# Attention, then a mixture of experts, on one core: the order of work inside a group of blocks is turned round

## The chip, the core and the metric

The kernel runs on one core of one Trainium2 chip. The metric is the device time of one execution in microseconds (us). The kernel before takes 1038.86 us (median of 3 runs, 1036.79 to 1040.83).

Five engines work side by side, each through its own queue in order: TensorE (PE in the profile, with PEld for its weight loads), VectorE (DVE), ScalarE (ACT), GpSimd (POOL) and SyncE (SP), which here only issues transfers (DMAs).

## What is computed

A transformer layer in fp32 on 2048 tokens of 128 numbers. The first half is causal attention with 16 heads of 64, the second a gated mixture of 8 experts with 2 chosen for each token, plus a shared expert. Cut to what matters here:

```python
x = L0_attn_x                                   # (1, 2048, 128)
qkv = einsum('bse,ehd->bshd', layernorm(x), qkv_w) + qkv_b
q, k, v = split(qkv, 3, axis=-1)
logits = where(causal, einsum('bqhd,bkhd->bhqk', q, k) / sqrt(64), large_negative)
probs  = softmax(logits, axis=-1)
attn   = einsum('bhqk,bkhd->bqhd', probs, v)
x = x + einsum('bqhd,hde->bqe', attn, out_w) + out_b
x = x + shared_ffn(layernorm(x)) + sum over the two best experts of weight * expert_ffn(layernorm(x))
```

## The kernel before, in words

**Pairs and steps.** Heads are taken in pairs j = 0 to 7. The 2048 query rows are taken in steps m = 0 to 7 of 256 rows: rows (128-row blocks) i = 2m and 2m+1. Within a pair the steps come in the order `turns` (L384): 2, 7, 0, 6, 1, 5, 3, 4. A step m has 2m+2 blocks of 128 keys.

**Scores.** `score_units` (L394) makes units of at most 512 keys for one row i and both heads. TensorE multiplies (L429, tile `sc`). VectorE scales or masks, writes `row` and takes the maximum (L440, and L444 for the last piece of a row), then the negative maximum `neg` (L458). ScalarE takes the exponential in place over the whole row (L461), one instruction for each head. I write sc_11_2 for the third unit of row 11, exp_11 for the two exponentials of row 11, neg_11 for its negative maximum.

**Turning the probabilities.** The product with V needs them transposed. There are two ways. Steps m = 4 to 7 are *by slabs* (L390): all but their last blocks are transposed within 32x32 squares by VectorE (L496), written to DRAM by SyncE (L500, tile `stage`) and read back (L514, tile `turned`); the last two or four blocks are turned by TensorE ahead of time into `tail` (`turn_last`, L527). All blocks of steps m = 0 to 3 are turned by TensorE: `turn` (L516) makes up to four transposes into one PSUM tile `tr` (L522), and ScalarE copies that to SBUF (L525, tile `pT`, six buffers). I write tr_0_1 for block 1 of step 0, and "the copy of tr_0_1" for that copy.

**Product, division, projection.** `times_v` (L547) multiplies one block with V into the accumulator `av` (L554). The sums of the exponentials are inverted (L480), transposed (L483, tile `inv`), and spread over 64 partitions by way of DRAM: GpSimd issues the write `invd` (L485) and, in `spread` (L562), the two reads `inb` (L567), which wait for the write. `divide` (L573) multiplies `av` by `inb` on VectorE (L575, tile `aT`). `project` (L578) multiplies `aT` by the output weights on TensorE (L581, tile `po`), and VectorE adds `po` to `xr` (L582). I write T:inv_0, inb_0, av_0, aT_0 and po_0 for those of step 0.

**Fill.** The projections to K, Q and V of the next pair are single units (`pq` L352 and `pv` L369) that are put between the rest from the queue `fill`. ScalarE moves K and V out of PSUM (L364, L376), VectorE Q (L362).

**PSUM.** All tiles but `av` come from one ring of six (tag "r"): a new `sc`, `tr`, `po`, `pq` or `pv` waits until the tile taken six places earlier has been read.

**What sets the order.** TensorE and VectorE work in the order in which the program is written (L614). ScalarE, GpSimd and SyncE are ordered by a planner when the kernel is built; the order is fixed from then on. The loop over steps (L665) splits each step into groups of blocks. A slab step has three groups: its tail, and two halves of the rest. Other steps have groups of three blocks. In each group the written order is:

1. a fill unit (steps that are not by slabs)
2. the turns of this group's blocks (`turned`, L533)
3. the projection of the step that ended before (`finish`, L656)
4. the product with V of the group *before* (kept in `last`); a slab step takes what is kept and its own blocks at once
5. a fill unit (slab steps), and slab transposes that are due (`turn_slabs`)
6. score units of a step that comes two or four steps later, by the counts in `runs`

Of the kernel before, what the change touches and what calls it, by code (L numbers as in the profile page):

```python
# [16 lines left out]
P = 128  # L17
# [6 lines left out]
def attention_then_moe(  # L24
# [58 lines left out]
    def load_wq(j, engine):  # L83
        wq_of[j] = norm.tile([P, 3, 2, D], F32, tag="wq", name=f"wq_{j}", bufs=3)
        engine.dma_start(wq_of[j], qkv_w[:, :, 2 * j : 2 * j + 2, :])
# [7 lines left out]
    with nc.allow_non_contiguous_dma(reason="1024 numbers"):  # L93
# [16 lines left out]
        fill=MASKED,  # L110
# [104 lines left out]
    def route_units(blocks):  # L215
# [34 lines left out]
        def turn_row(t0):  # L250
            part = blocks[t0 : t0 + 4]
            pt = psp.tile([P, 512], F32, tag="r", name=f"pt_{k0}_{t0}")
            for t, b in enumerate(part):
                nc.tensor.transpose(pt[:, ts(t, P)], row[:, t0 + t, :E], ident)
            for t, b in enumerate(part[::2]):
                nc.scalar.copy(zT[:, b * P : (b + 2) * P], pt[:, ts(t, 2 * P)])
            in_zT.update(part)
# [77 lines left out]
                    )  # L335
                    no_order("sent", ins)

        turns = [lambda t0=t0: turn_row(t0) for t0 in range(0, n, 4)]
        return [statistics, normed, None, *turns, None, logits, None, best1, best2, ranks]


    attn = tc.tile_pool(name="attn", bufs=2)
# [2 lines left out]
    def qkv_units(j):  # L345
        kT = pool.tile([P, S], F32, tag="kT", name=f"kT_{j}")
        qT = [None] * NG
        vt = pool.tile([P, NT, P], F32, tag="vt", name=f"vt_{j}")

        def qk_unit(s, n):  # L350
            pq = psp.tile([P, 512], F32, tag="r", name=f"pq_{j}_{s}_{n}")
            nc.tensor.matmul(  # L352
                pq,
                wq_of[j][:, s, :, :],
                xnT[:, ts(n, 512)],
                start=True,
                stop=True,
            )
            bias = bqk[:, s, j : j + 1]
            if s == 0:  # L360
                qT[n] = pool.tile([P, 512], F32, tag=f"qT{n}", name=f"qT_{j}_{n}", bufs=1)
                nc.vector.tensor_scalar_add(qT[n], pq, bias)  # L362
            else:
                nc.scalar.activation(kT[:, ts(n, 512)], pq, AF.Identity, bias=bias)  # L364

        def v_unit(g):
            pv = psp.tile([P, 4, P], F32, tag="r", name=f"pv_{j}_{g}")
            for t in range(4):
                nc.tensor.matmul(  # L369
                    pv[:, t, :],  # L370
                    xnT[:, ts(4 * g + t, P)],
                    wq_of[j][:, 2, :, :],
                    start=True,
                    stop=True,
                )
            nc.scalar.copy(vt[:, ts(g, 4), :], pv)  # L376

        q, k = ([lambda s=s, n=n: qk_unit(s, n) for n in range(NG)] for s in range(2))
        return (kT, qT, vt), q, k, [lambda g=g: v_unit(g) for g in range(NG)]
# [10 lines left out]
    def by_slabs(m):  # L390

        return (2 * m) // 4 * 4 if 2 * m >= NT // 2 else 0
# [78 lines left out]
    def turn_slabs(most, age=True, due=False):  # L471


        for t in to_turn:
            t[-1] -= age
        while to_turn and (to_turn[0][-1] < 0 or not (age or due)) and most:
            j, m, q, h, sums, _ = to_turn.popleft()
            if h == 1:
                inv = inv_of[j, m]
                nc.vector.reciprocal(inv[:, 2 * q : 2 * q + 2], sums)  # L480
                if q == 1:

                    nc.vector.transpose(inv, inv)  # L483
                    invd_of[j, m] = dram.tile([32, P], F32, tag=f"inv{m}", name=f"invd_{j}_{m}")
                    nc.gpsimd.dma_start(  # L485
                        invd_of[j, m].rearrange("n (a i) -> a n i", a=4),
                        inv,
                    )
            X = by_slabs(m) * 32
            if not X:  # L490
                continue
            most -= 1
            if q == 0 and h == 0:
                staged_of[j, m] = dram.tile([P, 16 * X], F32, tag=f"stage{m}", name=f"stage_{j}_{m}")
            row = rows_of[j, m][q][:, h, : 4 * X]
            nc.vector.transpose(row, row)  # L496
            row = row.rearrange("p (b x) -> p b x", b=4)
            to = staged_of[j, m].rearrange("(b i) (c x) -> i b c x", i=32, c=16)
            for a in range(4):
                ins = nc.sync.dma_start(to[:, :, 8 * q + 4 * h + a, :], row[ts(a, 32)])  # L500
                no_order(f"stage_{j}_{m}", ins)
# [106 lines left out]
    def scores_of(n):  # L608
        if n >= len(steps):
            return deque()  # L610
        j, m = steps[n]
        return deque(score_units(j, m, *qkv[j][0][:2]))
# [12 lines left out]
        u()  # L625
        turn_slabs(2)
    fill, later = deque(), deque()
    last = []
    ending = None

    shared_w = []
# [1 line left out]
    def load_shared():  # L633
        for k, w in enumerate((w_gate, w_up, w_down)):
            t = norm.tile([P, 3 * P], F32, tag="wq", name=f"shared_{k}", bufs=3)
            if k < 2:
                t = t[:, :F]
                nc.sync.dma_start(t, w[:, NE, :])
            else:
                t = t.rearrange("p (c e) -> p c e", c=NFC)  # L640
                for c, (f0, fn) in enumerate(FCH):
                    nc.sync.dma_start(t[:fn, c, :], w[f0 : f0 + fn, NE, :])
            shared_w.append(t)
# [18 lines left out]
                    blocks = [b for m in batch for b in (2 * m, 2 * m + 1)]  # L662
                    routes.append(deque(route_units(blocks)))

    for n, (j, m) in enumerate(steps):  # L665
        at = n % NM
        if at == 0 and j + 1 < NP:
            qkv[j + 1] = qkv_units(j + 1)


            _, q, k, v = qkv[j + 1]
            fill.extend([*k, q[3], *v])
            later.extend([q[1], q[0], q[2]])
            if j + 2 < NP:
                load_wq(j + 2, nc.sync)
            while j and blank:
                nc.sync.dma_start(blank.popleft(), mask[:, :ROW].unsqueeze(1).to_broadcast([P, 16, ROW]))
        if at == 0 and j == NP - 1:
            load_shared()
        if at == 5 and later:  # L680
            assert not fill
            fill.extend(later)
            later.clear()
        if at == 6 and j + 1 < NP:
            assert not fill
        near = by_slabs(m)
        coming = scores_of(n + (4 if near else 2))
        if n == 0:
            coming.extend(scores_of(3))

        if near:
            groups = [list(range(near, 2 * m + 2))]
            groups += [list(range(k, k + near // 2)) for k in range(0, near, near // 2)]
            runs = [3, 3, len(coming) - 6]
        else:
            groups = [list(range(k, min(k + 3, 2 * m + 2))) for k in range(0, 2 * m + 2, 3)]
            half = len(coming) // 2
            runs = {1: [len(coming)], 2: [2 * (half // 2), half], 3: [0, half, half]}[len(groups)]
        for k, group in enumerate(groups):
            if fill and not near:  # L700
                fill.popleft()()
            turn_slabs(1)
            now = [turned(j, m, b) for b in group]
            if k == 0:
                spread(j, m)
            if ending is not None:
                finish(*ending)
                ending = None
            route_on()
            ready, last = (last + now, []) if near else (last, now)  # L710
            for t in ready:
                jt, mt, b = t[:3]
                times_v(*t, qkv[jt][0][2])
                if b == (by_slabs(mt) or 2 * mt + 2) - 1:
                    assert ending is None
                    ending = (jt, mt, divide(jt, mt))
            if fill and near:
                fill.popleft()()
            turn_slabs(1, age=False, due=True)
            if near and k == 0 and n + 2 < len(steps):  # L720
                turn_last(*steps[n + 2])
            if n == 0 and k == 0:
                turn_last(*steps[1])
            if n == 0 and k == 1:
                load_turned(*steps[1])
            if near and k == 1 and n + 2 < len(steps):
                load_turned(*steps[n + 2])
            for _ in range(runs[k] if k < len(groups) - 1 else len(coming)):
                if coming:
                    coming.popleft()()  # L730
    assert not last
    finish(*ending)
    assert len(routes) == 2
    attn.__exit__(None, None, None)
# [309 lines left out]
```

## Time and profile before

| what | value |
|---|---|
| median of 3 runs | 1038.86 us (1036.79 to 1040.83) |
| the profiled execution | 1043.9 us, of which its span is 1042.2 us |
| mean granted TensorE clock | 0.971 |
| PE busy | 949.6 us (91%) |
| DVE busy | 745.1 us (71%) |
| ACT busy | 541.3 us (52%) |
| POOL busy | 211.3 us (20%) |
| DMA | 205.33 MB, mean 197 GB/s |

The span has three parts. Up to about 42 us the input is normalised and turned. From there to about 860 us the eight pairs follow, about 101 us each in the middle (one and the same wait of a score unit ends at 444.00 us in one pair and at 544.74 us in the next). The rest is the mixture of experts.

How to read it: "busy" for TensorE is made of records whose ends are modelled, so 99% does not say that it never waited. An idle time is shown in square brackets, with the engine and line that ended it. In rows of groups, "out<-in" are the program's names, and the count is in instructions as the hardware sees them (one fp32 matmul gives two records).

### The profile page before, as it was taken

What the parts mean: (1) busy time and instruction counts of PE and PEld (TensorE: products, weight loads), DVE (VectorE), ACT (ScalarE), POOL (GpSimd) and SP (SyncE); (2) the same over time, 40 slices, a digit from 0 to 9 for tenths busy, and PEclk for the clock granted to TensorE, in tenths of its full rate; (3) what the DMA queues carried; (4) which work ended last, traced back from release to release, by engine and by line L of the source; (5) the groups of instructions that cost most, each with busy time, mean ns of one, the idle gap of its engine ahead of it and who ended that gap; (6) DMA issues with size and microseconds to landing.
All of it is one profiled execution on the core that took longest, in us unless ns stands there. A gap on an engine that the chain in (4) does not pass through costs nothing. (4 is left out here: it accounts for less than half of the span.)

```text
span 1042.2 us, 18362 instructions
## 1 busy us (share of the span) xinstructions
PE 949.6 (91%) x5928; PEld 573.3 (55%) x5928; DVE 745.1 (71%) x2315; ACT 541.3 (52%) x1015; POOL 211.3 (20%) x404
## 2 busy tenths in 40 slices
PE   4987999999999999999999999999999788689995
PEld 2553545565556556555555555556555446357773
DVE  3764788778877877887778777876787675545553
ACT  4552546655655565456556554655465452315551
POOL 1030110121102111111111111111111112734441
PEclk9988999999999999999999999999999898889998
DMA  9996748774787478747866875677577751443104
GB/s 200 190 275 172 272 117 308 251 215 144 258 277 213 160 245 272 210 165 252 257 189 190 253 245 174 204 250 243 165 221 254 250 172 65 142 129 85 43 26 125
DMA packets 126736, 205.33 MB, mean 197 GB/s; under 512 B 16449, under 2 KB 119203, under 8 KB 122545
## 3 DMA queue, kind: packets, MB, share of 16 engines
q1 hardware_dynamic: 116496, 190.06, 59.9%
q0 software_dynamic: 8416, 13.82, 5.4%
q8 instruction: 48, 0.79, 0.3%
q10 hardware_dynamic: 1728, 0.27, 0.2%
q14 instruction: 48, 0.39, 0.1%
HBM read 105.10 MB, written 99.35 MB: 196 GB/s over the span
## 5 line engine op out<-in xcount | busy, mean ns | idle before, releaser
L461 ACT ACTIVATE row<-row,neg 128x1920 f32<-128x1920 f32 (+15 forms) x256 | 306.3, 1202 | 255.0 <-DVE neg L458 115.2
L440 DVE TENSOR_SCALAR_CACHE_REDUCE row<-sc 128x512 f32<-128x512 f32 x384 | 243.2, 684 | 97.9 <-PE sc L429 68.2
L429 PE MATMUL sc<-kT,qT 64*128 64x512 f32 (+3 forms) x1280 | 299.4, 557 | 14.1 <-DVE row L440 5.9
L429 PEld LDWEIGHTS sc<-kT,qT 64*128 64x128 f32 x1280 | 128.3, 188 | 149.9 <-issue 79.9
L496 DVE STREAM_TRANSPOSE row<-row 128x1024 f32<-128x1024 f32 (+1 forms) x128 | 190.3, 1490 | 0.8 <-ACT row L461 0.8
L554 PE MATMUL av<-turned,vt 128*64 128x256 f32 x1280 | 158.0, 395 | 0.0
L485 POOL DMA_DIRECT2D invd<-inv x64 | 46.0, 718 | 506.3 <-DVE inv L483 503.1
L444 DVE CUSTOM_DVE_ANT_0 row<-sc,mask 128x384 f32<-128x384 f32 (+3 forms) x256 | 114.8, 485 | 19.6 <-PE sc L429 19.0
L554 PEld LDWEIGHTS av<-turned,vt 128*64 128x64 f32 x1280 | 88.7, 140 | 63.5 <-issue 24.6
L522 PE MATMUL tr<-ident,row 128*128 128x128 f32 x896 | 119.2, 276 | 3.3 <-ACT pT L525 1.9
L522 PEld LDWEIGHTS tr<-ident,row 128*128 128x128 f32 x896 | 99.6, 141 | 36.3 <-issue 19.0
L567 POOL DMA_DIRECT2D inb<-invd x128 | 76.1, 603 | 146.0 <-DMA invd<-inv 133.4
L525 ACT COPY pT<-tr 128x512 f32<-128x512 f32 (+1 forms) x160 | 79.0, 553 | 31.9 <-PE tr L522 31.9
L554 PE MATMUL av<-pT,vt 128*64 128x256 f32 (+1 forms) x640 | 79.6, 372 | 6.4 <-ACT pT L525 6.1
L352 PE MATMUL pq<-xnT,wq 128*128 128x512 f32 x128 | 72.0, 650 | 2.4 <-DVE row L440 2.4
L581 PE MATMUL po<-wo,aT 128*128 128x128 f32 x256 | 44.2, 297 | 26.0 <-DVE row L440 19.7
L554 PEld LDWEIGHTS av<-pT,vt 128*64 128x64 f32 x640 | 38.7, 136 | 47.9 <-issue 18.3
L581 PEld LDWEIGHTS po<-wo,aT 128*128 128x128 f32 x256 | 34.7, 197 | 44.1 <-DVE row L440 36.3
L525 ACT COPY tail<-tr 128x512 f32<-128x512 f32 x96 | 43.6, 520 | 16.7 <-PE tr L522 16.7
L949 POOL DMA_INDIRECT ybuf<-yo,to x39 | 38.3, 982 | 62.2 <-ACT yo L948 59.1
L461 ACT ACTIVATION_READ_ACCUMULATOR row<-row,neg 128x1 f32 x256 | 49.7, 194 | 0.0
L575 DVE TENSOR_TENSOR aT<-av,inb 128x256 f32<-128x256 f32 x64 | 26.5, 415 | 27.5 <-DMA inb<-invd 15.2
(169 smaller groups left out, 894.9 us busy)
## 6 DMA issues: line engine op xcount, KB each, us to landing
stage<-row SPq DMA_DIRECT2D x256, 192.0 KB, 3.8
turned<-stage SPq DMA_DIRECT2D x16, 3072.0 KB, 10.7
stage<-row SPq DMA_DIRECT2D x256, 128.0 KB, 2.6
turned<-stage SPq DMA_DIRECT2D x16, 2048.0 KB, 8.8
zbuf<-mask SPq DMA_DIRECT2D x8, 1056.0 KB, 19.2
inb<-invd POOLq DMA_DIRECT2D x128, 64.0 KB, 3.4
zs<-zbuf SPq DMA_DIRECT2D x39, 66.0 KB, 1.9
yt<-ybuf SPq DMA_DIRECT2D x4, 512.0 KB, 4.3
```

What stands on the lines that cost most here:

```text
L352: nc.tensor.matmul(pq, wq_of[j][:, s, :, :], xnT[:, ts(n, 512)], start=True, stop=True,)
L429: nc.tensor.matmul(sc[:, :cw], qT[i // 4][hd, ts(i % 4, P)], keys, start=True, stop=True)
L440: nc.vector.tensor_scalar(dst, src, SCALE, None, ALU.mult, ALU.max, accum_out=mh)
L444: nc.vector.tensor_tensor_reduce(out=rows[:, h, c0 : c0 + cw], in0=scs[h][:, :cw], in1=mask[:, 512 - cw : 512], scale=SCALE, scalar=-F32_M ...
L461: nc.scalar.activation(row, row, AF.Exp, bias=neg[:, h : h + 1], accum_out=sums[:, h : h + 1])
L485: nc.gpsimd.dma_start(invd_of[j, m].rearrange("n (a i) -> a n i", a=4), inv,)
L496: nc.vector.transpose(row, row)
L522: nc.tensor.transpose(tr[:, h, ts(q, P)], rows_of[j, m][q][:, h, ts(b, P)], ident)
L525: nc.scalar.copy(dst[:, :, q0 * P :], tr[:, :, q0 * P :])
L554: nc.tensor.matmul(av_of[j, m][hd, q0 * P :], vt[:, b, hd], pT[:, h], start=(b == near), stop=(b == (near or 2 * m + 2) - 1),)
L567: nc.gpsimd.dma_start(inb[h * D : (h + 1) * D, :].rearrange("d (q p) -> d q p", q=2), row.partition_broadcast(D),)
L581: nc.tensor.matmul(po[:, q, :], aT[:, ts(q, P)], wo[:, j, :], start=True, stop=True)
```

## The change

The order within a group is turned round. A group now does, in this order: the product with V of *its own* blocks, which were turned in the group before; the projection of the step that ended before; a fill unit; slab transposes that are due; the turns of the *next* group's blocks; the score units. The projection comes ahead of the product only where the group is its step's only one (step 0) or its last. Groups are cut anew: steps 0, 1, 2 and 3 have groups of 2, 2, 3 and 4 blocks (before 2, 3+1, 3+3 and 3+3+2), so at most four blocks are turned ahead. The score units are dealt out by `runs_of`. The number and the shapes of instructions stay as they are, except that the routing's `turn_row` units, which were two list entries, become one.

The core of the diff:

```diff
+    def groups_of(m):
+        near, width = by_slabs(m), 2 * m + 2
+        if near:
+            return [range(near, width), range(near // 2), range(near // 2, near)]
+        step = {2: 2, 4: 2, 6: 3, 8: 4}[width]
+        return [range(k, k + step) for k in range(0, width, step)]
+
+    def runs_of(m, units):
+        if by_slabs(m):
+            return [3, 3, units - 6]
+        return [units] if m == 0 else [2 * (units // 4), units - 2 * (units // 4)]
+
+    def turned_group(i):
+        n, _, group = groups[i]
+        return [turned(*steps[n], b) for b in group]
...
-        for k, group in enumerate(groups):
-            if fill and not near:
-                fill.popleft()()
-            turn_slabs(1)
-            now = [turned(j, m, b) for b in group]
-            if k == 0:
-                spread(j, m)
-            if ending is not None:
-                finish(*ending)
-                ending = None
-            route_on()
-            ready, last = (last + now, []) if near else (last, now)
-            for t in ready:
-                jt, mt, b = t[:3]
-                times_v(*t, qkv[jt][0][2])
-                if b == (by_slabs(mt) or 2 * mt + 2) - 1:
-                    assert ending is None
-                    ending = (jt, mt, divide(jt, mt))
-            if fill and near:
-                fill.popleft()()
-            turn_slabs(1, age=False, due=True)
+        turn_slabs(1)
+
+        before, ending = ending, None
+        ends = group[-1] == (near or 2 * m + 2) - 1
+        if before is not None and ends:
+            finish(*before)
+        for t in now if not near else turned_group(i):
+            times_v(*t, qkv[j][0][2])
+        if ends:
+            ending = (j, m, divide(j, m))
+        elif before is not None:
+            finish(*before)
+        route_on()
+        if fill:
+            fill.popleft()()
+        turn_slabs(1, age=False, due=True)
+        if i + 1 < len(groups) and not by_slabs(steps[groups[i + 1][0]][1]):
+            now = turned_group(i + 1)
```

The tail turns of slab steps, the loads of `turned` and the score units follow at the end of the group as before.

More of the change, by code (lines that the diff above doesn't have):

```diff
@@ L336, in ranks, with turn_rows @@
                     no_order("sent", ins)
-        turns = [lambda t0=t0: turn_row(t0) for t0 in range(0, n, 4)]
-        return [statistics, normed, None, *turns, None, logits, None, best1, best2, ranks]
+        def turn_rows():
+            for t0 in range(0, n, 4):
+                turn_row(t0)
+        return [statistics, normed, None, turn_rows, None, logits, None, best1, best2, ranks]
     attn = tc.tile_pool(name="attn", bufs=2)
@@ L627, in attention_then_moe @@
     fill, later = deque(), deque()
-    last = []
     ending = None
@@ L663, in finish @@
                     routes.append(deque(route_units(blocks)))
-    for n, (j, m) in enumerate(steps):
-        at = n % NM
[L667 to L698, printed above, removed]
-        for k, group in enumerate(groups):
-            if fill and not near:
-                fill.popleft()()
-            turn_slabs(1)
-            now = [turned(j, m, b) for b in group]
-            if k == 0:
-                spread(j, m)
-            if ending is not None:
-                finish(*ending)
-                ending = None
-            route_on()
-            ready, last = (last + now, []) if near else (last, now)
-            for t in ready:
-                jt, mt, b = t[:3]
-                times_v(*t, qkv[jt][0][2])
-                if b == (by_slabs(mt) or 2 * mt + 2) - 1:
-                    assert ending is None
-                    ending = (jt, mt, divide(jt, mt))
-            if fill and near:
-                fill.popleft()()
-            turn_slabs(1, age=False, due=True)
[L720 to L730, printed above, removed]
@@ L731, in attention_then_moe @@
-    assert not last
+    def groups_of(m):
[8 more added lines that the diff above has]
+        return [units] if m == 0 else [2 * (units // 4), units - 2 * (units // 4)]
+    groups = [(n, k, g) for n, (_, m) in enumerate(steps) for k, g in enumerate(groups_of(m))]
@@ new lines, in turned_group @@
+    def turned_group(i):
+        n, _, group = groups[i]
+        return [turned(*steps[n], b) for b in group]
+    now = turned_group(0)
+    for i, (n, k, group) in enumerate(groups):
+        j, m = steps[n]
+        near = by_slabs(m)
+        at = n % NM
+        if k == 0:
+            if at == 0 and j + 1 < NP:
+                qkv[j + 1] = qkv_units(j + 1)
+                _, q, key, v = qkv[j + 1]
+                fill.extend([*key, q[3], *v])
+                later.extend([q[1], q[0], q[2]])
+                if j + 2 < NP:
+                    load_wq(j + 2, nc.sync)
+                while j and blank:
+                    clear = mask[:, :ROW].unsqueeze(1).to_broadcast([P, 16, ROW])
+                    nc.sync.dma_start(blank.popleft(), clear)
+            if at == 0 and j == NP - 1:
+                load_shared()
+            if at == 5 and later:
+                assert not fill
+                fill.extend(later)
+                later.clear()
+            if at == 6 and j + 1 < NP:
+                assert not fill
+            coming = scores_of(n + (4 if near else 2))
+            runs = runs_of(m, len(coming))
+            if n == 0:
+                coming.extend(scores_of(3))
+                runs = [len(coming) // 2] * 2
+            spread(j, m)
+        turn_slabs(1)
[15 more added lines that the diff above has]
+            now = turned_group(i + 1)
+        if near and k == 0 and n + 2 < len(steps):
+            turn_last(*steps[n + 2])
+        if n == 0 and k == 0:
+            turn_last(*steps[1])
+        if n == 0 and k == 1:
+            load_turned(*steps[1])
+        if near and k == 1 and n + 2 < len(steps):
+            load_turned(*steps[n + 2])
+        for _ in range(runs[k]):
+            if coming:
+                coming.popleft()()
+        if k == len(runs) - 1:
+            assert not coming
```

## The prediction

> **What bounds the kernel now.** I read the page's slices first, then what TensorE waited for, then the timeline of one pair in the middle (440 to 545 us), engine by engine.
>
> ```profile
> PE   4987999999999999999999999999999788689995
> DVE  3764788778877877887778777876787675545553
> ACT  4552546655655565456556554655465452315551
> PEclk9988999999999999999999999999999898889998
> ```
>
> From slice 5 to 31, the eight pairs, TensorE is at 9 in every slice, VectorE at 7 to 8 and ScalarE at 5 to 6. TensorE sets the end, so only time in which it waits, or the work itself, counts. The answer on TensorE's waits shows how little it waits openly:
>
> ```profile
> PE po L581 <- DVE row L440: 19.7, 10, 5.8
> PE av L554 <- ACT pT L525: 6.1, 7, 1.0
> PE sc L429 <- DVE row L440: 5.9, 2, 3.4
> PE sc L429 <- ACT tail L525: 5.6, 8, 0.7
> ```
>
> (us in total, times, longest.) Since matmul ends are modelled, part of the waiting lies inside "busy". I compare each block's start-to-start time with the same block where it runs freely: a score unit of 512 takes 0.85 us, one of 128 0.21, one block of av about 0.46, a tr of four transposes 0.43, po 0.54, pq 0.96, pv 0.95. So four places in a pair lose time: sc_14 behind tr_4 (541.56 to 546.07: 4.5 for 2.55 us of work), sc_8 before po_0 (516.25 to 520.13: 3.9 for 1.9), av_2 (1.3) and sc_12 behind tr_7 (1.2). Together 6.4 of 101 us: no reordering can win more than about that, 51 us over eight pairs.
>
> Now the place that decides, step 0, from the timelines of VectorE, GpSimd, TensorE and ScalarE:
>
> ```profile
> 507.20 0.21 DVE L483 STREAM_TRANSPOSE inv<-inv 128x32 f32<-128x32 f32 x1
> ...
> 517.61 0.42 DVE L575 TENSOR_TENSOR aT<-av,inb 128x256 f32<-128x256 f32 x1 [1.71 <-DMA inb<-invd]
> ```
>
> ```profile
> 507.71 0.70 POOL L485 DMA_DIRECT2D invd<-inv  x1 [9.77 <-DVE inv L483]
> 514.33 2.37 POOL L567 DMA_DIRECT2D inb<-invd  x4 [5.93 <-DMA invd<-inv]
> ```
>
> ```profile
> 507.43 1.12 PE L352 MATMUL pq<-xnT,wq 128*128 128x512 f32 x2
> ...
> 520.13 0.71 PE L581 MATMUL po<-wo,aT 128*128 128x128 f32 x4 [0.98 <-DVE row L440]
> ```
>
> ```profile
> 507.10 1.58 ACT L461 ACTIVATE row<-row,neg 128x1536 f32<-128x1536 f32 x1 [3.68 <-issue]
> 508.68 1.56 ACT L461 ACTIVATE row<-row,neg 128x1536 f32<-128x1536 f32 x1
> 510.23 0.57 ACT L376 COPY vt<-pv 128x512 f32<-128x512 f32 x1
> 510.70 0.86 ACT L525 COPY pT<-tr 128x512 f32<-128x512 f32 x2
> ```
>
> The reader is to see: T:inv_0 at 507.20, inb_0 usable at 517.6, a round trip of 10.4 us (9.7 to 11 in the pairs I looked at). Already now aT_0 waits 1.71 us for it, though it stands behind four score reads and three slab transposes. And exp_11 runs straight through, the copies of tr_0 behind it.
>
> **The change, part by part.** The work is unchanged: same matmuls, copies and transfers. GpSimd's and SyncE's queues keep their order; the slab transposes of rows 14 and 15 come about a group (7 us) later, and their `stage` writes with them, but `turned` of step 7 now lands at 486.2 and is first multiplied at 498.1, so that is hidden at no cost (with that cover gone, it would be 7 us a pair). One routing entry less costs nothing. What changes is distance.
>
> *Gap 1, tr to av.* Before, a group's copies have the previous group's product, its scores, a fill and the next turns as cover (about 5 us). After, only the scores of one group, and for tr_0, tr_1_0/1 and tr_2_3..5 none, as those groups' counts in `runs` come out as zero. *Gap 2, av to po* is longer or the same for steps with two groups, but for step 0, T:inv_0 to aT_0 shrinks from about 8 us of VectorE work to 2.8. I walk through the pair with the rows' durations, in the orders of the built kernel.
>
> *Stretch C, step 0 into 6.* Start: av_7 ends at 507.43. TensorE: pq 0.96, tr_0 0.66, po_7 0.54, first av_0 block, at 510.1. ScalarE now has the copy of tr_0_0 ahead of exp_11 and that of tr_0_1 behind it. The first waits for tr_0_0 (508.9), so exp_11 starts at 509.4 instead of 507.1, ends at 512.6, and the copy is there at 513.1: TensorE waits 3.0 us. Then av_0, pv_0, sc_2, sc_3, the tail of av_6: po_0 at 516.8. aT_0 cannot be done before 517.6 + 0.43 = 518.0: 1.2 us more. Queued behind aT_0 on VectorE are T:row_10 (1.2), the reads of sc_2 and sc_3 (2.3), T:row_11 (1.2) and the add of po_0. The PSUM ring waits for those: the tr_5 tiles take the places of sc_2 and sc_3 (free from 519.8 to 521.6), sc_8_0 that of po_0 (523.4). Then the copies of tr_5, behind exp_3, let sc_8 end at 525.9. Before, the same work ended at 520.77: **+5.1 us**, its old wait of 1.9 already taken off.
>
> Here the Trainium skill speaks for the change: "DMA: Bandwidth & Descriptors", section on the anatomy of one DMA, gives a transfer a fixed cost of about 2 us plus its bytes. Two small ones in a row with 1.3 us of issue would be an estimated 5.4 us; aT_0 would never wait, and C would cost 0.8 us. The row says 10.4, because `invd` alone takes 6 us while `turned` of step 6 is being read (502.5 to 513.6). I take the row.
>
> *D, step 6:* VectorE catches up, -0.2.
>
> *Stretch E, step 1 into 5.* In the built order exp_9 stands behind the move of pv_3 and ahead of the copies of tr_1. From av_6's end: pv_3 0.99, its move 0.55, exp_9 2.75, copies 0.5 each: av_1's second block at 5.35 us where TensorE stood ready at 2.4. **+2.95**, and sc_14's wait behind tr_4 stays: **+3.1** together.
>
> *Stretch A, steps 5, 3, 4.* exp_15 (4 us from neg_15, 459.9) stands ahead of the copies of tr_3_4..7. Their cover is tr_3 and sc_4_0 only; sc_4_1 needs the place of tr_3_4: 2.0 us. Then sc_12_0 needs po_3's place, whose add stands behind T:row_15 on VectorE: 3.0 instead of 1.2, partly given back in sc_13: **+1.6**. *B, steps 2 and 7:* the copies of tr_2_3..5 come behind exp_13, 2.0 instead of 1.3 at av_2, aT_2 waits for inb_2 without hurting TensorE: **+0.3**. Both bounds of A+B: 0 (if earlier waits shift ScalarE enough) and 3; the nearest row, av_2's existing wait behind exp_13 at just this place, is well met by the same walk, so I keep 1.9.
>
> *Clock.* In no row of before does TensorE lose as much in one place, so this cost is bounded from both sides. In one pair it did lose something like it:
>
> ```profile
> 619.46:622.87 3.41, 1.75 (x14) 1.23 (x14) 3.38 (x10) 0.00 (x0) 0.85 (x2) 0.98 0.56 139
> 622.87:626.28 3.41, 3.41 (x18) 1.94 (x16) 1.36 (x8) 2.26 (x3) 0.00 (x0) 0.52 0.70 161
> ```
>
> (Stretch, length, busy us of PE, PEld, DVE, ACT, POOL, then granted clock.) After 3.41 us with TensorE at 51% the clock was halved for the next 3.41; the 24 av records took 4.43 instead of 2.74: 1.7 us. By "TensorE: Matmul & The Clock Gate", section on HAM oscillation, only idle gaps over about 3.4 us cool the clock; my waits are each shorter, so by the page it is 0. The row shows less suffices. In C, from 516.8 to 523.4, TensorE is at some 48%. Bounds 0 and 1.7 in a pair (below nothing is excluded: waiting can't raise a clock already at 1.00); as half of the slow work may fall into waits, I take 0.85.
>
> **Sum.** C occurs in all 8 pairs: 41. A+B+D+E = 1.9 - 0.2 + 3.1 = 4.8, in the 7 that still make scores for a next pair: 34. Clock 0.85 in the 6 pairs at full clock: 5. Together +80 us. Against the profiled execution: 1043.9 + 80 = 1124. That one is 5 us above the median, so on the median of the runs: 1038.9 + 80, about **1118**.
>
> **Rivals.**
> - *Only aT_0 counts.* The late copies heal, because a TensorE that waits gives ScalarE (58% busy) time to catch up. For it: its idle 42%. Against it: the copies stand behind particular exponentials, not behind a backlog. 8 x 5.1 = 41: 1080. Chance 0.21.
> - *More waits, and the clock with them:* three halved windows in each of the 6 pairs, 31 us instead of 5, gives 1144; A at its upper bound another 8. Chance 0.15.
> - *Faster: the projection leaves the shadow of the scores.* po now stands right behind a product, so the waits of sc_8 and po_0 (1.9), av_2 (1.3) and sc_12 (1.2) go: 4.4 x 8 = 35, 1004. It decides if the round trip of inb_0 is under 5.4 us: po_0 would be reached at 513.0 without waits. All I looked at took 9.7 or more. Chance 0.06.
> - *It does nothing:* ScalarE's order brings back the old distances. The built order speaks against it. 1039, chance 0.03.
>
> **How the numbers follow.** The likeliest case, 1118, has 0.55. A measurement of this kernel can tell about 0.5% from no change. Slower 0.91, same 0.03, faster 0.06. The range runs from 1062 (C at three fifths) to 1146.
>
> **What would show it.** After: aT_0 with an idle time of 4 us or more ended by inb; av ended by ACT pT with far more than 6.1 us, in steps 0, 1 and 2; a pair of some 111 us; TensorE below 92% in the middle slices, with 8s in the clock row. I am wrong if inb_0 arrives sooner than 8 us after T:inv_0, or if av of steps 0 and 1 doesn't wait for copies.

## The result, and the profile after

The changed kernel takes 1187.36 us (median of 4 runs, 1180.86 to 1192.04), the kernel before in the same job 1039.84 us (1036.79 to 1044.77). The ratio (of the means) is 1.1409, with a 95% interval of 1.1338 to 1.148: slower by 147 us, where +80 was forecast. The time lies outside the range of the forecast, 1062 to 1146. The profiled execution took 1187.54 us, its span 1185.8 us (before 1042.2), at a mean granted clock of 0.937 (before 0.971). In the changed program all lines from 429 to 581 stand three further down: L429 is L432, L525 is L528, L554 is L557, L575 is L578.

The page's slices, three of the rows shown of before:

```profile
PE   5887898889888988899879888998889878789995
DVE  4676676667666766677557755776567655564553
PEclk9998899999998999899999998999999989878998
```

TensorE has 8s and 7s all through the pairs, VectorE went from 7 and 8 to between 5 and 7, and 8s stand in the clock row, as the forecast said they would. No engine took over as the bound: VectorE is busy 63% of the span (before 71%), ScalarE 46% (before 52%). What TensorE waited for (us in total, times, longest):

```profile
PE av L557 <- ACT pT L528: 54.6, 23, 3.0
PE po L584 <- DVE aT L578: 20.2, 15, 5.2
```

The product's wait for copies went from 6.1 to 54.6 us, the projection now waits for its own division (20.2 us, before 5.0), and the old wait of po for the queue of VectorE (19.7) is gone from the list. The division's group, before and after (busy us, mean ns, then the idle time before it and what ended it):

```profile
L575 DVE TENSOR_TENSOR aT<-av,inb 128x256 f32<-128x256 f32 x64 | 26.5, 415 | 27.5 <-DMA inb<-invd 15.2
L578 DVE TENSOR_TENSOR aT<-av,inb 128x256 f32<-128x256 f32 x64 | 26.0, 407 | 118.8 <-DMA inb<-invd 101.9 <-PE av L557 10.0 <-PE sc L432 6.7
```

The idle time went from 27.5 to 118.8 us; the part that inb ended went from 15.2 to 101.9.

I compared one pair in the middle block by block, from the start of pv_3 to the next (428.95 to 529.69 us before, 366.81 to 489.92 us after), cut at the prediction's stretches:

| stretch | before, us | after, us | difference | forecast |
|---|---|---|---|---|
| E: pv_3 to the first `turned` block of av_5 | 17.02 | 23.33 | +6.3 | +3.1 |
| A: pq_0_2 (the third `pq` of step 5) to the end of av_4 | 27.04 | 29.50 | +2.5 | +1.6 |
| B: end of av_4 to the first `turned` block of av_7 | 17.73 | 23.48 | +5.8 | +0.3 |
| C: end of av_7 to the first `turned` block of av_6 | 13.34 | 21.20 | +7.9 | +5.1 |
| D and the rest | 25.6 | 25.6 | 0.0 | -0.2 |
| the pair | 100.74 | 123.1 | +22.4 | +9.9, and 0.85 of clock |

The pair shown is a little dearer than the mean: from the issue of `invd` of step 2 at 187.2 us to the one six pairs later at 919.6 a pair takes 122.1 us, before 101.3 (178.5 to 786.4).

Stretch E shows how such a loss is made up. ScalarE at this place before, two of its rows:

```profile
430.63 1.57 ACT L525 COPY pT<-tr 128x512 f32<-128x512 f32 x3
432.06 1.39 ACT L461 ACTIVATE row<-row,neg 128x1280 f32<-128x1280 f32 x1
```

And after, the timelines of ScalarE and TensorE:

```profile
368.00 0.59 ACT L379 COPY vt<-pv 128x512 f32<-128x512 f32 x1 [3.11 <-PE pv L372]
368.48 1.36 ACT L464 ACTIVATE row<-row,neg 128x1280 f32<-128x1280 f32 x1
...
369.84 1.35 ACT L464 ACTIVATE row<-row,neg 128x1280 f32<-128x1280 f32 x1
...
371.18 1.05 ACT L528 COPY pT<-tr 128x512 f32<-128x512 f32 x2
```

```profile
371.80 1.98 PE L557 MATMUL av<-pT,vt 128*64 128x256 f32 x8 [2.97 <-ACT pT L528]
373.71 1.23 PE L584 MATMUL po<-wo,aT 128*128 128x128 f32 x4
```

Before, the copies came ahead of exp_9. Now it is the move of pv_3, exp_9, and only then the two copies: the order that the prediction read, and the wait of 2.97 us that it named (2.95). The rest of the +6.3 is behind it: po takes 1.23 us where it takes 0.71 at full clock, av 1.98 where it takes 0.87. The stretches of 3.41 us around it (length, busy us of PE, PEld, DVE, ACT, POOL, then granted clock, DMA share, GB/s):

```profile
367.95:371.36 3.41, 0.89 (x9) 0.65 (x6) 0.55 (x1) 3.36 (x6) 0.50 (x1) 0.96 0.63 147
371.36:374.77 3.41, 2.97 (x13) 1.83 (x14) 0.00 (x0) 0.88 (x2) 2.01 (x5) 0.50 0.31 93
374.77:378.18 3.41, 3.41 (x13) 2.08 (x13) 1.64 (x4) 0.86 (x2) 0.00 (x0) 0.54 0.17 38
378.18:381.59 3.41, 3.41 (x22) 1.33 (x20) 3.38 (x10) 0.92 (x1) 0.00 (x0) 1.00 0.45 116
```

TensorE was busy 0.89 of 3.41 us while it waited, and then worked for 6.8 us at half clock. The wait cost 2.97 us, and what followed it up to 3.4 more (half of 6.8).

Not every wait is followed by this. The 1.94 us that av_2 waits at 437.63, shown below, fall mostly into a stretch with TensorE busy for 1.77 of 3.40 us (436.00 to 439.40), and the next stretch stayed at full clock. In the trace the clock changes in steps of 3.41 us. Between 150 and 950 us of the changed kernel every step at full clock in which TensorE was busy for less than 49% was followed by half clock, and none in which it was busy for more than 61%; in between both occur. Other runs have exceptions on both sides (a step at 42% that kept the clock, one at 79% that did not), and busy times have modelled ends, so this is a tendency and no rule.

Stretch B, forecast at +0.3, from the timelines of VectorE, GpSimd and TensorE:

```profile
429.56 0.21 DVE L486 STREAM_TRANSPOSE inv<-inv 128x32 f32<-128x32 f32 x1
...
443.10 0.42 DVE L578 TENSOR_TENSOR aT<-av,inb 128x256 f32<-128x256 f32 x1 [7.22 <-DMA inb<-invd]
```

```profile
430.07 0.70 POOL L488 DMA_DIRECT2D invd<-inv  x1 [7.64 <-DVE inv L486]
436.83 2.52 POOL L570 DMA_DIRECT2D inb<-invd  x4 [6.06 <-DMA invd<-inv]
```

```profile
437.63 1.36 PE L557 MATMUL av<-pT,vt 128*64 128x256 f32 x12 [1.94 <-ACT pT L528]
...
443.58 0.71 PE L584 MATMUL po<-wo,aT 128*128 128x128 f32 x4 [1.02 <-DVE aT L578]
```

The same two issues before:

```profile
481.01 0.70 POOL L485 DMA_DIRECT2D invd<-inv  x1 [10.15 <-DVE inv L483]
486.63 2.37 POOL L567 DMA_DIRECT2D inb<-invd  x4 [4.92 <-DMA invd<-inv]
```

T:inv_2 at 429.56, inb_2 usable at 443.1: a round trip of 13.5 us. The small write `invd` is issued while `turned` of step 7 (3 MB) is read, from 427.04 us on, and GpSimd waits 6.06 us for it, before 4.92. The reads issued from 436.83 on, two of them for inb_2, then took 5.2 us to land (median of four), before 4.3; `stage` writes are issued at about that time in both (from 435.91 on, before from 486.93). How much each of the large transfers slows the small ones was not tested by itself. VectorE stands still for 7.2 us, as the work behind aT_2 waits in order: po_2 comes late, and the scores of rows 0 and 1, written at 439.97, are read from 445.19 on.

The clock: between 150 and 950 us the kernel before has 6 stretches at half clock (37.5 us together, one of them inside the steady pairs), the changed one 17 (71.7 us), two to four a pair. Over the whole span the clock withheld 30.5 us of full-speed time before and 74.6 after (the span times one minus the mean granted clock): up to 44 of the 147 us, since part of it falls into waits.

### The profile page after: what moved, and what is told of

Its sections match the earlier page's. It is cut to its first block, busy times and chain, and to the rows that moved or that the text cites. A ratio compares the mean times of both kernels' runs of the same rounds, so it can differ in the third digit from the quotient of the medians.

```text
span 1185.8 us, 18359 instructions
## 1 busy us (share of the span) xinstructions
PE 1016.2 (86%) x5928; PEld 599.9 (51%) x5928; DVE 743.2 (63%) x2315; ACT 546.2 (46%) x1017; POOL 211.2 (18%) x404
## 5 line engine op out<-in xcount | busy, mean ns | idle before, releaser
L432 PE MATMUL sc<-kT,qT 64*128 64x512 f32 (+3 forms) x1280 | 331.1, 587 | 32.4 <-ACT pT L528 10.0
L432 PEld LDWEIGHTS sc<-kT,qT 64*128 64x128 f32 x1280 | 139.8, 198 | 180.1 <-issue 64.0
L557 PE MATMUL av<-turned,vt 128*64 128x256 f32 x1280 | 152.1, 384 | 0.0
L525 PE MATMUL tr<-ident,row 128*128 128x128 f32 x896 | 127.6, 287 | 12.5 <-ACT pT L528 4.2
L557 PE MATMUL av<-pT,vt 128*64 128x256 f32 (+1 forms) x640 | 85.6, 402 | 54.6 <-ACT pT L528 54.6
L525 PEld LDWEIGHTS tr<-ident,row 128*128 128x128 f32 x896 | 106.7, 147 | 47.0 <-issue 15.1
L557 PEld LDWEIGHTS av<-turned,vt 128*64 128x64 f32 x1280 | 86.3, 137 | 72.8 <-issue 26.3
L528 ACT COPY pT<-tr 128x512 f32<-128x512 f32 (+1 forms) x160 | 77.2, 543 | 66.1 <-PE tr L525 65.9
L578 DVE TENSOR_TENSOR aT<-av,inb 128x256 f32<-128x256 f32 x64 | 26.0, 407 | 118.8 <-DMA inb<-invd 101.9
L557 PEld LDWEIGHTS av<-pT,vt 128*64 128x64 f32 x640 | 42.2, 145 | 94.4 <-ACT pT L528 66.9
L584 PE MATMUL po<-wo,aT 128*128 128x128 f32 x256 | 50.3, 324 | 20.3 <-DVE aT L578 20.2
L585 DVE TENSOR_TENSOR xr<-xr,po 128x256 f32<-128x256 f32 x64 | 25.7, 402 | 62.5 <-PE po L584 62.5
L528 ACT COPY tail<-tr 128x512 f32<-128x512 f32 x96 | 45.0, 513 | 33.7 <-PE tr L525 33.4
L379 ACT COPY vt<-pv 128x512 f32<-128x512 f32 x32 | 18.6, 581 | 72.2 <-PE pv L372 72.2
```

Of the source, the lines that this page charges most:

```text
L432: nc.tensor.matmul(sc[:, :cw], qT[i // 4][hd, ts(i % 4, P)], keys, start=True, stop=True)
L525: nc.tensor.transpose(tr[:, h, ts(q, P)], rows_of[j, m][q][:, h, ts(b, P)], ident)
L528: nc.scalar.copy(dst[:, :, q0 * P :], tr[:, :, q0 * P :])
L557: nc.tensor.matmul(av_of[j, m][hd, q0 * P :], vt[:, b, hd], pT[:, h], start=(b == near), stop=(b == (near or 2 * m + 2) - 1),)
L584: nc.tensor.matmul(po[:, q, :], aT[:, ts(q, P)], wo[:, j, :], start=True, stop=True)
```

## The experiments

Each run was measured beside the kernel before, whose median lay between 1036.21 and 1049.49 us from job to job, so ratios compare better than microseconds.

**The theories.** *Theory 1*: the copies of turned blocks stand behind exponentials, TensorE waits, the clock halves. *Theory 2*: aT waits for inb, and VectorE and the PSUM ring with it. *Theory 3*: both, about half each, because turns, product and division come a group sooner against the scores. *The cut*: not the order but the new groups and counts. *Theory 4*, formed from the first eight of these runs, is below.

**The old cut in the new order.** Groups of three and the counts of the kernel before:

```diff
-        step = {2: 2, 4: 2, 6: 3, 8: 4}[width]
-        return [range(k, k + step) for k in range(0, width, step)]
+        return [range(k, min(k + 3, width)) for k in range(0, width, 3)]
...
```

> The new order, but with the groups and score counts cut as before (3+1, 3+3, 3+3+2 blocks instead of 2+2, 3+3, 4+4). Theory 1 (order: av waits for late copies of its turned blocks, then the clock is halved): the waits sit in steps 0, 1 and 2, whose distances hardly change with the cut, so 1187 within 10 us. Rival (cut: turning four blocks at once overfills the PSUM ring): a good part of the 147 us comes back, 1120 or less.

1168.61 us, ratio 1.1266 (1.1229 to 1.1303). The cut is 1.4 points of the 14.1, with an interval from about 0.3 to 2.5: a small part, so the rival fell. Theory 1's 1187 within 10 us was missed too. (The next expectation calls this run e_cut.)

**The old cut, and the next group's turns ahead of the product.**

```diff
+        mine = now
+        if i + 1 < len(groups) and not by_slabs(steps[groups[i + 1][0]][1]):
+            now = turned_group(i + 1)
...
-        for t in now if not near else turned_group(i):
+        for t in mine if not near else turned_group(i):
...
```

> As e_cut, but the next group's blocks are turned ahead of the group's own product instead of behind it; product, projection, fill, division and scores stay in the new order. Theory 1 (late copies, and the halved clock that follows them): the 55 us of open waits of av go and about half of the halved clock with them, 75 to 95 us less than e_cut, about 1100. Theory 2 (the early aT waits for inb over DRAM, and the copies' waits only stand in front of that): the wait moves to po, at most 20 us less than e_cut.

1162.13 us, ratio 1.1211 (1.1174 to 1.1248). This gives each copy a product as cover, and it takes the wait for copies away, but hardly any time. TensorE's waits:

```profile
PE po L584 <- DVE aT L578: 43.7, 17, 5.9
PE tr L525 <- ACT pT L528: 35.5, 15, 3.3
...
PE av L557 <- ACT pT L528: 9.2, 7, 1.3
```

av waits 9.2 us instead of 74.9 (in the run with the old cut); the time went to the projection and to the PSUM places of the turns. The 6.5 us won are what Theory 2 had said (at most 20). Theory 1 alone fell.

**VectorE copies the turned blocks of steps 0 to 3, in the changed kernel.**

```diff
-            turn(j, m, b, pT)
+            turn(j, m, b, pT, nc.vector.tensor_copy)
```

> The changed kernel, but VectorE instead of ScalarE copies the turned blocks of steps 0 to 3 out of PSUM, so no exponential stands ahead of a copy; distances stay. Theory 1: 1090 to 1120 (160 copies of some 0.55 us come onto VectorE, 88 us, of which part falls into its waits). Theory 2: 1170 or more, since aT stays where it is and VectorE has more to do.

1137.38 us, ratio 1.0974 (1.0937 to 1.101). Taking the copies from behind the exponentials is worth 4.4 points; Theory 1's range was missed upwards, Theory 2's downwards.

**The same in the kernel before**, as a control:

> The kernel before with the copies of the turned blocks of the first four steps on VectorE, the edit that made the changed kernel about 4 points faster. If that gain was the cost of copies that the change put behind exponentials, it gives nothing or a loss here, as the kernel before waits only 6 us for these copies and VectorE is the fuller engine: 1035 to 1070. If copies are cheaper on VectorE whatever the order: 1010 or less.

1056.8 us, ratio 1.0086 (1.0059 to 1.0114): a small loss. So the gain in the changed kernel is not that VectorE copies better. It comes with the change's order, in which the copies stand behind exponentials.

**Useless matmuls in the waits.** 9 of 128 x 128 ahead of av_0 and 12 ahead of av_1, into the place of `av`:

```diff
+    WARM = {1: 12, 0: 9}
...
+        if k == 0 and m in WARM:
+            av_of[j, m] = psp.tile([P, 256], F32, tag="av", name=f"av_{j}_{m}", bufs=2)
+            for _ in range(WARM[m]):
+                nc.tensor.matmul(av_of[j, m][:, :P], ident, ident, start=True, stop=True)
```

> The changed kernel plus useless matmuls (128x128 by 128, into the accumulator before its first real product) ahead of av_0 (9) and av_1 (12) in each pair, some 2 and 2.6 us of work at full clock, in the place of waits of 2 and 3 us. If the halved clock behind these waits costs TensorE time (some 5 us a pair by the clock records): 25 to 40 us faster, 1147 to 1162. If the lost clock lies in other waits: 1187 or some us more.

1165.97 us, ratio 1.1255 (1.1213 to 1.1298). More work, and 1.5 points faster than the change (by the two intervals 0.4 to 2.7): 11 stretches at half clock instead of 17, and 52.7 us withheld over the span instead of 74.6. So halved clock is a cause of its own in this kernel, not only a mark of waiting. The range of 1147 to 1162 was missed by 4 us.

**inb from a constant**, without the division by the sums, in the changed kernel, and then in the kernel before:

```diff
-            row = invd_of[j, m][:4].rearrange("(q h) p -> h q p", h=2)[h]
+            row = flat[:4].rearrange("(q h) p -> h q p", h=2)[h]
```

> The changed kernel, but inb is read from a small buffer in DRAM written once at the start (ones) instead of from invd, so aT never waits for the round trip; the division by the sums is left out of the result. Theory 3 (in the new order the product comes a group sooner against the scores, so both the copies behind the exponentials and inb behind T:inv are late, each about half of the loss): 1115 to 1140. Theory 2 (inb is the main cause): 1090 or less. Theory 1 (copies are the main cause): 1165 or more.

> The same edit in the kernel before, as a control: its aT waits 15 us in all for inb, most of it in steps 0 of the pairs. All theories: 1020 to 1036.

1147.47 us, ratio 1.0966 (1.0927 to 1.1006); in the kernel before 1035.33 us, ratio 0.9885 (0.9852 to 0.9918). The round trip is worth 4.4 points in the changed kernel and 1.1 before, so the change made 3.3 points of it. Theory 2 alone fell. Theory 3's range was missed by 7 us, which is as much as the kernel before took longer in that job (1047.21 us).

**Both together.**

> Both edits in the changed kernel: VectorE copies the turned blocks, and inb does not hang on invd. Theory 3: nearly all of the loss is gone, 1045 to 1080. If a third wait is behind (slab transposes and their writes, the PSUM ring): 1090 or more.

1091.09 us, ratio 1.0411 (1.0375 to 1.0448): 10.0 points of the 14.1 go with these two waits (by the two controls the same edits are worth some 0.3 points in the kernel before), and a third wait is left. VectorE's waits show it:

```profile
DVE row L445 <- DMA stage<-row: 56.5, 28, 6.7
```

(In this kernel the lines stand two further down still.) The reads of scores wait for a row's buffer, which the staging of the slab rows has not yet given free: 27.0 us before, 38.9 in the change, 56.5 here, where little else is in the way.

**Both together, and the old cut**, with which the slab transposes of rows 14 and 15 come a group sooner:

> The changed kernel with three things at once: VectorE copies the turned blocks of the first four steps, inb is read from a constant (the division by the sums is left out), and groups are cut at three blocks with the score counts of the kernel before, so that the slab transposes of rows 14 and 15 come a group sooner. With the first two alone it was 1091. If the late staging of rows 14 and 15 (scores of rows 12 and 13 behind it) is what is left: 1055 to 1075. If something else is left: 1085 or more.

1080.16 us, ratio 1.0305 (1.0258 to 1.0352), with 40.1 us of that wait left. One more point. The expectation of 1055 to 1075 was missed: three points are left, and what makes them was not tested piece by piece.

**The division behind the scores**, in the changed kernel:

```diff
-        if ends:
-            ending = (j, m, divide(j, m))
-        elif before is not None:
+        if before is not None and not ends:
             finish(*before)
...
         if k == len(runs) - 1:
             assert not coming
+        if ends:
+            ending = (j, m, divide(j, m))
```

> The changed kernel with aT written at the end of the group, behind its scores, instead of right behind the product, so VectorE reads the scores before it waits for inb. Theory 2: VectorE's 102 us of waiting for inb no longer hold up the PSUM ring, 30 to 60 us faster, 1130 to 1157. Theory 3: po waits longer instead and the copies stay late, 1165 to 1195.

1172.54 us, ratio 1.1186 (1.1146 to 1.1227), as Theory 3 had it. aT's idle time falls from 118.8 to 20.1 us, and the time by 2.2 points only: the wait moved to TensorE, where po waits 70.7 us for aT instead of 20.2. Theory 2's 1157 was missed: moving the division back in VectorE's queue did not make inb land sooner.

**Theory 4, the shift.** It says that all these waits have one root. Count the groups as g. In the short steps (0 to 3) the kernel before writes scores(g), turns(g+1), product(g), scores(g+1). The change writes product(g), turns(g+1), scores(g). As a cycle the two differ little; but against the scores, and so against all that is tied to them (the exponentials, the inverted sums, the slab transposes), turns, product and division now come a whole group sooner. If this is the cause, putting only the scores back should undo the loss, whatever the order in the group.

**Scores in front of each group**, in the new order, and with the turns ahead of the product:

```diff
         turn_slabs(1)
+        for _ in range(runs[k]):
+            if coming:
+                coming.popleft()()
...
-        for _ in range(runs[k]):
-            if coming:
-                coming.popleft()()
```

> Theory 4 (the shift): not the order inside a group costs the time, but that turns, product and division of a step now run a group (some 7 us of TensorE) sooner against the score units, and so against the exponentials, T:inv and the slab transposes, which are tied to the scores. This kernel has the new order in the cycle (product, projection, fill, turns, scores), but each group's score units stand in front of its product, which shifts every score one group sooner; the work is the same. Theory 4: the waits of aT for inb and of the staging go, the copies keep half of their trouble, because the turns still come right after an exponential: about 1095 (1060 to 1130). Theory 1 (copies alone): the copies have no more cover than before, 1165 or more. If the order in the cycle is what counts: within 1170 to 1200.

> The turns of the next group ahead of its own product, at most three blocks at a time, as in the kernel before, and each group's scores in front of it: this brings back the distances of the kernel before between scores, turns and product, while projection and fill stay where the change put them, behind the product. Theory 4 (the shift): 1030 to 1055. If projection and fill behind the product cost something by themselves: 1080 or more. It differs from the kernel measured at 1162 (turns ahead of the product, the old cut) only in the place of the scores.

1356.11 us, ratio 1.2951 (1.2887 to 1.3015), and 1297.66 us, ratio 1.2397 (1.2324 to 1.247): far off. VectorE's waits in the second:

```profile
DVE row L443 <- DMA stage<-row: 116.3, 28, 7.0
```

The built order told why: in the long steps the kernel before has the scores *behind* the product, as the change has. My edit moved those too, so they came a group sooner than ever and found their row buffers not yet staged. So the distance is bound on the other side as well, and these two runs did not test what I meant.

**The distances of the kernel before, projection and fill as in the change.** Short steps: scores, turns of the next group, product. Long steps: product, scores. `give` issues the score units:

```diff
+        if not near:
+            give()
+            turn_slabs(1)
...
+            now = turned_group(i + 1)
         before, ending = ending, None
...
+        if near:
+            give()
```

> The order of the kernel before between turns, products and scores, exactly (in the short steps scores, turns of the next group, product; in the long steps product, scores; groups of three), and of the change only this: projection and fill stand right behind a product and not behind turns or scores. Theory 4 (the shift against the scores is what costs): within 2% of before, 1020 to 1060. If the places of projection and fill cost: 1090 or more.

1108.67 us, ratio 1.0591 (1.0563 to 1.062): by the letter the second expectation. TensorE's waits and a piece of its timeline:

```profile
PE po L584 <- DVE aT L578: 71.5, 25, 8.1
...
PE av L557 <- ACT pT L528: 6.1, 7, 1.0
```

```profile
492.61 0.82 PE L557 MATMUL av<-tail,vt 128*64 128x256 f32 x8
497.13 0.71 PE L584 MATMUL po<-wo,aT 128*128 128x128 f32 x4 [3.71 <-DVE aT L578]
```

The copies wait as little as before, to the tenth of a microsecond. What is left is po of a short step, which in this kernel stands only one tail block (0.8 us) behind its own division. In the change the score units of a group lie between as well, so I took this for a cost of my kernel and not yet for an answer. It took two more.

**The kernel before with the shift alone.** As the run with the turns ahead of the product, but each projection ahead of the next product:

```diff
-        if before is not None and ends:
+        if before is not None:
             finish(*before)
...
-        elif before is not None:
-            finish(*before)
```

> The kernel before with the shift alone: turns, product and scores in its cyclic order and groups of three, but the scores of the short steps one group later, so that turns and product run a group sooner against them; projections stand behind the next turns as in the kernel before. Theory 4 (the shift makes the loss): 1105 to 1165. If the places of projection and fill or the turns behind the product make it: 1060 or less.

1175.05 us, ratio 1.1239 (1.1215 to 1.1262): with the order of the kernel before inside the group, the shift alone makes a loss as large as the change with the old cut. That is 10 us above Theory 4's range, and far from the 1060 of its rival. The copies have cover here (av waits 9.6 us for them); the loss shows as po behind aT, 66.7 us, and as turns without a PSUM place, 37.1 us.

**The changed order with the shift alone undone.** As the run before last, but with the turns behind the product, and po of a short step behind the scores of the next long one:

```diff
-            else:
-                now = turned_group(i + 1)
...
-        if before is not None and ends:
+        if before is not None and not (near and k == 0):
             finish(*before)
+            before = None
-        for t in mine if not near else turned_group(i):
+        for t in now if not near else turned_group(i):
             times_v(*t, qkv[j][0][2])
...
         if near:
             give()
+            if before is not None:
+                finish(*before)
...
+        if short:
+            now = turned_group(i + 1)
```

> The changed order of the cycle, product, turns, scores, with groups of three, but the scores of the short steps one group sooner, which undoes the shift; projections come with at least three score units, or a group of turns and scores, behind their division. It has the turns behind the product, as the change put them. Theory 4: 1030 to 1065, since only the cover of the copies of a group is shorter, by one product. If turns behind the product cost by themselves: 1090 or more.

1050.29 us, ratio 1.0049 (1.0027 to 1.0071), inside Theory 4's range. The same place as stretch E, ScalarE and then TensorE:

```profile
425.22 1.57 ACT L528 COPY pT<-tr 128x512 f32<-128x512 f32 x3
426.65 1.39 ACT L464 ACTIVATE row<-row,neg 128x1280 f32<-128x1280 f32 x1
```

```profile
427.64 0.71 PE L584 MATMUL po<-wo,aT 128*128 128x128 f32 x4
428.28 1.52 PE L557 MATMUL av<-pT,vt 128*64 128x256 f32 x12
```

The copies are again ahead of exp_9, and av_1 starts without a wait. With po behind score units and the turns behind the product, the loss of the run before last is gone too.

| kernel | order in a short step's group | scores of the short steps | ratio to before |
|---|---|---|---|
| before | scores, turns, product | as before | 1 |
| shift undone | scores, product, turns | as before | 1.0049 (1.0027 to 1.0071) |
| shift alone | turns, product, scores | a group later | 1.1239 (1.1215 to 1.1262) |
| change with the old cut | product, turns, scores | a group later | 1.1266 (1.1229 to 1.1303) |
| the change | product, turns, scores, cut anew | a group later | 1.1409 (1.1338 to 1.148) |

With either order inside the group the distance to the scores is worth 12 points. At either distance the order comes out at half a point or less, where the intervals allow up to 0.7 at the old distance and about 0.9 at the new one. (The projections and the fill do not stand at quite the same places in the four kernels with groups of three. The waits of the run at 1.0591 suggest that this costs points where a projection stands right behind its division, which it does in none of the four.) No version came out below the kernel before with all its work done.

## Why the prediction was wrong in size and right in kind

**Right.** The cost came by the way that the prediction gave: "What changes is distance". The copies of steps 0, 1 and 2 came behind the exponentials named, aT_0 waited 8.17 us for inb_0, TensorE fell to 86% of the span with 8s in the clock row, and stretch D cost nothing. In stretch E the wait itself was forecast at 2.95 and measured at 2.97 us. The rival on the other side, the projection out of the shadow of the scores, had its point at a round trip under 5.4 us; the two traced here were 11.2 (inb_0, 461.33 to 472.51) and 13.5 us. The rival of "more waits, and the clock with them", 1144, was the nearest, and still short.

**Wrong: the clock, "I take 0.85".** The pair shown has 13.65 us at half clock, up to 6.8 us of loss. Over the span up to 44 us more than before were lost to it, where the sum had 5. I had both bounds from a single disturbance (0 and 1.7) and took the middle, though my own walk put three waits of 2 to 3 us and more into each pair, and the row that I quoted said what one of them does. The Trainium skill's "TensorE: Matmul & The Clock Gate", section on HAM oscillation, speaks of idle gaps over about 3.4 us; the longest wait of av for a copy here was 3.0, and the clock fell all the same. The measurement decides: a stretch of 3.41 us with 26% busy was followed by two at half clock. The useless matmuls show that this is a cause and how much of it could be had back that way: 1.5 points. The step that failed is the price of a wait: its own length and almost nothing behind it.

**Wrong: B, "aT_2 waits for inb_2 without hurting TensorE: +0.3".** It was +5.8. The round trip was taken as that of before, but T:inv_2 now falls 2.5 us behind the start of the 3 MB read (427.04 to 429.56), where before it fell 4.8 us behind (475.68 to 480.50), so more of that read lay ahead of `invd` (6.06 us of waiting for it, before 4.92), and the reads of inb took longer too, for a reason that stays open. And a wait of 7.2 us on VectorE is not harmless: of TensorE's open waits in B, 1.02 us (po_2), 0.36 and 0.76 stood behind aT_2. Another 0.60 and 1.94 were for copies, where before there were 0.98.

**Wrong: "that is hidden at no cost".** The later slab transposes of rows 14 and 15 were checked against `turned` of step 7 only. They also take VectorE's time, and they give the row buffers free into which the scores of later rows are read. The transposes of row 15 now run from 415.81 to 419.86, when sc_12 is already being written (before, they ended at 468.17 and sc_12 began at 470.06). VectorE reads sc_12 from 420.27 on, and TensorE needs 3.71 us for sc_12_3 and the first two units of sc_13, before 2.14. Then VectorE waits 2.21 us, to 426.92, for `stage` before it can read sc_13. T:inv_2 and exp_13 stand behind that, so part of the loss of B starts here. With copies and round trips out of the way it was the largest wait of VectorE, 56.5 us.

**Wrong in size: C and E.** C was +7.9 for +5.1, with both its waits there (av_0 1.90, po_0 1.84, and 0.69 more at po_7 for aT_7), and two half stretches, 466.7 to 470.1 and 473.5 to 476.9. E was +6.3 for +3.1; the excess is about what its half clock can cost (3.4). A was +2.5 for +1.6.

By the pair, the stretches came to +22.4 where their forecast was +9.9. Of the 12.5 us between, C and E have 6.0, and all the half clock of this pair lies in these two (at most 6.8 us); B has 5.5, A 0.9, D 0.2. A walk that takes a block's duration from a full-speed pair and adds the waits one by one leaves out that a wait can make the next blocks slower and that the small transfers fall at another moment. The exact share of the clock stays open, as the records do not tell a slow matmul that was hidden from one that was not. (Two readings of the slices were loose and bear on none of this: in slices 5 to 31 VectorE has a 6, and ScalarE four 4s.)

## What to carry to other kernels

In a kernel with several in-order queues, do not ask only which step stands behind which in a loop body: ask against what it is shifted, around the whole cycle, and list all that is tied to the thing it moved against. Here the order inside the group was worth about half a point and one group of distance 12. The right distance is bound on both sides (a group later and the copies and divisions wait, a group sooner in the long steps and the row buffers do), so move one class of steps at a time. And when a walk finds several waits of 2 to 3 us in a kernel that keeps TensorE at 9 tenths, look at how busy TensorE is in the 3.41 us around each of them. Where that falls to half or less, as in E here, price what follows at half clock, not only the wait.

## What the runs showed of the hardware that I had not expected

- The clock halves without a long idle. 3.41 us with 0.89 us of matmul work, no wait longer than 3.0, were followed by 6.8 us at 0.5. How busy TensorE was in the step of 3.41 us told it in this kernel: under 49% always half, over 61% never (150 to 950 us). Twenty-one useless matmuls a pair made the whole kernel 1.5 points faster.
- Two small dependent transfers took 13.5 us (inb_2) where the same sizes took 10.4 us in the kernel before (inb_0). The wait for the write is nearly the same in the two (6.06 and 5.93 us, each beside a 3 MB read); from the first issue of the reads to their use it is 6.3 us against 3.3. What held the reads up stays open.
